# Softmax denominators of the masked layers: two products with ones instead of eight transposes and a reduction

## The chip, the cores and the metric

The kernel runs on one core of a Trainium2 chip. The metric is the time of one launch on the device, in microseconds, as the median of three runs. Beside it stands one profiled execution, from which all rows, waits and timelines below are taken.

The core has a matrix engine (TensorE; PE in the profile, PEld for its weight loads), a vector engine (VectorE, DVE), a scalar engine (ScalarE, ACT), GpSimd (POOL) and a queue engine (SyncE, SP) that issues transfers. SBUF is the on-chip memory of 128 partitions, PSUM the accumulator memory in which TensorE leaves its results.

## The reference

Four cross-attention layers run in a row on 2048 queries of 256 channels, all attending to the same 1601 context rows of 512. Layers 0, 2 and 3 are masked, with 16 heads of 64; layer 1 is grouped, with 16 query heads of 16 on 4 key heads. Each masked layer computes

```python
logits = jnp.einsum('bhqd,bhkd->bhqk', q, k) * scale
logits = logits + col_bias[None, None, :, :]
probs = jax.nn.softmax(logits, axis=-1)
out = jnp.einsum('bhqk,bhkd->bhqd', probs, v)
out = out.transpose(0, 2, 1, 3).reshape(B, HW, HEADS * HEAD_DIM)
out = out @ Wo + bo
out = out + residual
```

`col_bias` lowers a few key columns for the queries that a mask leaves out. The denominator of the softmax is the sum over the 1601 keys of the exponentials, one number for each query and head. All is in 32-bit floats.

## The kernel before, in words

**Tiling.** A unit of a masked layer is two heads and 512 queries (`QB`). Its scores are kept with the keys on the partitions: 13 chunks (`NT`) of up to 128 keys, each chunk a tile of 128 partitions by 2 heads by 512 queries. A masked layer has 8 pairs of heads (a block, with its weights) by 4 groups of queries, so the three masked layers have 96 units. The grouped layer has 4 blocks by 4 groups, and works differently: it makes its scores twice and gets its denominators from a column of ones in the values.

**The steps of a masked unit.** For each chunk, `masked_scores` (L713) makes the scores in a PSUM tile `s`, ScalarE copies it to a tile `p` in SBUF (L725), and VectorE takes the running maximum over the chunks (L730). After the last chunk `maxima` turns the maxima by eight transposes (L773), reduces them on VectorE (L774), and sends them by way of DRAM to all partitions. Five steps later the exponentials begin: VectorE subtracts the maximum (L804), ScalarE takes the exponential (L809), and GpSimd adds the chunk to the tile `sums` (L812, L814), 128 partitions by 2 heads by 512 queries. Two steps behind that, TensorE multiplies with the values into the PSUM tile `po` (L849), the two heads side by side in 64 columns each.

**After the last values** the unit needs its denominators, on all partitions, to divide `oT`, the evicted `po`. `denominators` (L887 to L898) takes a PSUM tile of the scores' pool, transposes `sums` into it in eight pieces, so that queries stand on the partitions and the 128 partial sums along the row, reduces that on VectorE (L891) and takes the reciprocal (L892). Then `on_all_partitions` writes the columns to DRAM (L676) and reads them back as rows broadcast to 64 partitions for each head (L679) into the tile `by`. `divide` multiplies on GpSimd (L912), and `project` multiplies with Wo on TensorE (L920) and adds the result to `xs` on VectorE (L932).

**PSUM.** The pool of the score tiles has two tiles of two banks each while masked layers run. A third tile (`b`) holds the subtracted maxima, one bank is `po`, and one bank (`pm`, here the shared bank) serves all the pieces that make keys, values and queries. Where the grouped layer is being exponentiated, the scores' pool is six single banks instead.

**The order of the work.** The program is written out step by step, two steps (a pair) at a time, and TensorE, ScalarE and VectorE keep the written order; GpSimd and SP are put in order by a scheduler when the program is built. In a pair stand the subtractions, the scores of two chunks, the exponentials, the values of two chunks, and then the pieces of `Pieces`. A piece has a cost and a flag `shared` (it uses the shared bank). Some pieces are due at a fixed number of steps after a unit's last values (`finish`); the others, which make the next block's keys and values, fill pairs:

```python
        def pair(self, steps, pairs):

            cost, taken = self.own(steps)
            many = len(self.fill) + len(self.later) > pairs
            while self.fill and not taken and (many or not cost):
```

A due piece with a cost keeps fillers out of its pair unless many are left; a shared one keeps them out always. The denominators, the division and the projection of a masked unit are due 2, 5 and 10 steps after its last values. SP issues nearly all transfers, in one order: context slices (L262), weights (L440), x (L703), and the two legs of `on_all_partitions` for the denominators and for the maxima.

Of the kernel before, what the change touches and what calls it, by code (L numbers as in the profile page):

```python
# [10 lines left out]
FP = mybir.dt.float32  # L11
# [3 lines left out]
ALU = mybir.AluOpType  # L15
AX = mybir.AxisListType
PSUM = bass.MemoryType.PSUM

P = 128
QB = 512  # L20
# [6 lines left out]
Piece = namedtuple("Piece", "run cost shared", defaults=(True,))  # L27
# [7 lines left out]
def tile_cross_attention_stack(ctx: ExitStack, tc: tile.TileContext, t: dict, out: bass.AP):  # L35
# [31 lines left out]
    nc = tc.nc  # L67
# [6 lines left out]
    NB = S // QB  # L74
    QT = QB // P
# [13 lines left out]
    work = ctx.enter_context(tc.tile_pool(name="work", bufs=2))  # L89
    small = ctx.enter_context(tc.tile_pool(name="small", bufs=2))  # L90
    dram = ctx.enter_context(tc.tile_pool(name="dram", bufs=1, space=bass.MemoryType.DRAM))
    ps_o = ctx.enter_context(tc.tile_pool(name="ps_o", bufs=1, space=PSUM))
    ps_m = ctx.enter_context(tc.tile_pool(name="ps_m", bufs=1, space=PSUM))
    scores_pools = ctx.enter_context(ExitStack())

    ident = const.tile([P, P], FP, name="ident")
    make_identity(nc, ident)
    ones = const.tile([P, P], FP, name="ones")
# [39 lines left out]
    psum = Scores()  # L138
# [351 lines left out]
    class Grouped:  # L490
# [5 lines left out]
        name = "L1_xattn_"  # L496
# [168 lines left out]
    def columns(q):  # L665


        return slice(q, QB, QT)

    def on_all_partitions(cols, to):  # L670


        n = cols.shape[1]
        rows = dram.tile([4, P, QT], FP, name="cols", bufs=4)[:n]
        with nc.allow_non_contiguous_dma(reason="1024 values, four at a time"):
            nc.sync.dma_start(out=rows.rearrange("h p q -> p h q"), in_=cols)  # L676
        for tile_, heads_ in to:
            src = rows[heads_].rearrange("(o h) p q -> o (h p q)", o=1)
            nc.sync.dma_start(out=tile_, in_=src.to_broadcast(tile_.shape))  # L679


    class Unit:
# [191 lines left out]
        def last(self):  # L874
            return self.sub == len(self.layer.SUBS) - 1

        def denominators(self):

            rden = small.tile([P, len(self.pair), QT], FP, name="rden")
            if self.masked:  # L880
                h = 0
                for pt in psum.heads(False)[0]:
                    of = range(h, h + pt.shape[1])
                    pt = pt.rearrange("p h (q k) -> p h q k", k=P)
                    for h in of:
                        for q in range(QT):
                            nc.tensor.transpose(  # L887
                                pt[:, h - of[0], q, :], self.sums[:, h, columns(q)], ident
                            )
                    h += 1  # L890
                    nc.vector.tensor_reduce(rden[:, of[0] : h, :], pt, AX.X, ALU.add)  # L891
                nc.vector.reciprocal(rden, rden)  # L892
            else:
                nc.vector.reciprocal(rden, self.dens)
            self.by = work.tile([P, QB], FP, name="by", bufs=1)
            on_all_partitions(
                rden,
                [(self.by[self.rows(h)], slice(h, h + 1)) for h in range(len(self.pair))],  # L898
            )
# [74 lines left out]
        def finish(self):  # L974

            if self.very_last:
                return [(0, Piece(lambda: self.quarters(of[len(units) - 2]), 2.0))]
            if self.final:

                found = [  # L980
                    (4 if self.b == NB - 2 else 2, Piece(self.denominators, 1.0, False)),
                    (7, Piece(self.divide, 0.0)),
                ]
                if self.b < NB - 2:
                    found.append((10 - 2 * self.b, Piece(self.project_rows, 2.0, False)))
                return found
            if not self.masked:
                return [
                    (1, Piece(self.den_columns, 0.0)), (3, Piece(self.denominators, 0.0)),
                    (6, Piece(self.divide, 0.0)), (8, Piece(self.project, 2.0, False)),  # L990
                ]
            return [
                (2, Piece(self.denominators, 1.0, False)), (5, Piece(self.divide, 0.0)),
                (10, Piece(self.project, 2.0, False)),
            ]


# [4 lines left out]
    for b in range(NB):  # L1002
        nc.scalar.dma_start(
            out=x_rows[b], in_=x[0, ts(b, QB), :].rearrange("(n p) c -> p n c", p=P)
# [10 lines left out]
    of = {}  # L1015
# [343 lines left out]
```

## Time and profile before

| What | us |
|---|---|
| Median of three runs | 4742.91 (4740.15 to 4749.87) |
| Profiled execution, its own time | 4745.24 |
| Span of that execution, first to last instruction | 4743.5 |
| TensorE busy in the span | 4596.3 (97%) |
| VectorE busy | 3744.2 (79%) |
| ScalarE busy | 3226.5 (68%) |
| GpSimd busy | 2977.4 (63%) |

The granted TensorE clock was 0.992 over the span. A row of a group of instructions gives its line, engine and operation, the tiles that it writes and reads (out<-in), its shape and count, then its busy time in us and the mean duration of one in ns, and after the last bar the idle time of that engine just before such instructions with what ended it. In a timeline the columns are start and duration in us, engine, line, operation, tiles, shape and how many of them are merged; brackets give idle time ahead of the row and what ended it. TensorE's ends are modelled and its matmuls overlap, so times on it are best read from start to start.

### The profile page before, as it was taken

How to read it: one execution, taken by the hardware profiler on the slowest of the kernel's cores; microseconds unless marked ns; L12 is line 12 of the kernel's file. 1: busy time of each engine (PE TensorE's matmuls, PEld its weight loads, DVE VectorE, ACT ScalarE, POOL GpSimd, SP SyncE). 2: the span in 40 equal slices, each digit the busy share in tenths (PEclk: the TensorE clock that was granted, in tenths of full speed). 3: DMA queues.
4: the chain of work that ended last, by engine and by line, in shares of the span. 5: the costliest groups of instructions: out<-in, count | busy, mean ns of one | idle time of the engine just before them, and what ended most of it. 6: DMA issues, size and time to landing. Idle time of an engine off the chain costs nothing.

```text
span 4743.5 us, 64047 instructions
## 1 busy us (share of the span) xinstructions
PE 4596.3 (97%) x23943; PEld 1914.1 (40%) x23943; DVE 3744.2 (79%) x3768; ACT 3226.5 (68%) x4013; POOL 2977.4 (63%) x1436
## 2 busy tenths in 40 slices
PE   8999999999989999999999999999999999999998
PEld 5444444444433333343444444344444444444433
DVE  5888888888876666653788888888888888888887
ACT  4777777777635555555677777777777777777776
POOL 3777777778730000000677777777777777777787
PEclk9999999999989999999999999999999999999999
DMA  4322323222201010021232232222232223232211
GB/s 150 85 84 79 88 77 86 81 80 78 74 27 38 20 29 21 20 61 39 79 89 84 78 89 78 84 80 82 76 91 73 86 81 85 75 86 77 84 36 39
DMA packets 349892, 337.63 MB, mean 71 GB/s; under 512 B 116421, under 2 KB 305381, under 8 KB 349580
## 3 DMA queue, kind: packets, MB, share of 16 engines
q1 hardware_dynamic: 346310, 328.14, 24.6%
q8 instruction: 189, 3.10, 0.3%
q0 software_dynamic: 1152, 3.28, 0.2%
q10 hardware_dynamic: 2118, 2.10, 0.1%
q14 instruction: 123, 1.01, 0.1%
HBM read 318.49 MB, written 14.69 MB: 70 GB/s over the span
## 4 chain that ended last, share of the span: by engine, by line
PE 87%; DVE 10%; issue 1%; ACT 1%; POOL 0%; DMA 0%; another core or an unknown queue 0%; ACTq 0%; DVEq 0%; POOLq 0%
PE po L849 28%; PE s L713 20%; PE t L744 9%; PE pm L413 7%; PE pm L459 6%; PE pm L483 4%; PE s L920 4%; DVE rden L891 2%; PE s L887 2%; DVE ntop L774 2%; DVE xs L932 2%; PE s L773 2%; DVE top L730 1%; DVE p L804 1%; PE t L819 1%
## 5 line engine op out<-in xcount | busy, mean ns | idle before, releaser
L814 POOL TENSOR_TENSOR sums<-sums,p 128x1024 f32<-128x1024 f32 x1145 | 2711.0, 2368 | 736.8 <-ACT p L809 566.0
L725 ACT COPY p<-s 128x1024 f32<-128x1024 f32 (+1 forms) x1248 | 1234.2, 1014 | 655.3 <-PE s L713 567.6
L804 DVE TENSOR_TENSOR p<-p,b 128x1024 f32<-128x1024 f32 (+1 forms) x1248 | 1461.2, 1210 | 55.5 <-ACT b L799 54.4
L849 PE MATMUL po<-p,v 128*64 128x512 f32 (+3 forms) x8320 | 1493.5, 522 | 4.9 <-ACT p L809 2.6
L730 DVE TENSOR_TENSOR top<-s,top 128x1024 f32<-128x1024 f32 (+1 forms) x1056 | 1291.4, 1223 | 234.1 <-ACT p L725 171.3
L713 PE MATMUL s<-q,kT 64*128 64x512 f32 (+1 forms) x4992 | 1336.7, 629 | 85.9 <-DVE ntop L774 23.2
L809 ACT ACTIVATE p<-p 128x1024 f32<-128x1024 f32 (+1 forms) x1248 | 1254.7, 1057 | 43.8 <-DVE p L804 42.6
L849 PEld LDWEIGHTS po<-p,v 128*64 128x64 f32 (+3 forms) x8320 | 365.7, 125 | 1115.8 <-issue 889.3
L713 PEld LDWEIGHTS s<-q,kT 64*128 64x128 f32 (+1 forms) x4992 | 388.6, 181 | 722.7 <-issue 215.5
L831 ACT ACTIVATE p<-t 128x512 f32<-128x512 f32 (+1 forms) x760 | 413.8, 594 | 297.6 <-PE t L819 256.5
L757 DVE TENSOR_REDUCE row_top<-t 128x1 f32<-128x512 f32 x700 | 451.2, 686 | 196.8 <-PE t L819 165.2
L912 POOL TENSOR_TENSOR oT<-oT,by 128x512 f32<-128x512 f32 x111 | 141.6, 1276 | 656.4 <-DMA by<-cols 336.1
L819 PE MATMUL t<-q,kT 32*128 32x512 f32 (+1 forms) x1520 | 489.1, 643 | 0.0
L744 PE MATMUL t<-kT,q 32*128 32x512 f32 (+1 forms) x1880 | 481.9, 553 | 0.0
L413 PEld LDWEIGHTS pm<-wv,ct 128*128 128x128 f32 (+1 forms) x2600 | 300.4, 187 | 130.4 <-issue 69.0
L413 PE MATMUL pm<-wv,ct 128*128 128x128 f32 (+2 forms) x2600 | 333.3, 281 | 1.7 <-ACT vs L417 0.7
L459 PE MATMUL pm<-ct,wk 128*128 128x256 f32 (+1 forms) x1344 | 316.7, 379 | 5.4 <-ACT ct L284 4.3
L774 DVE TENSOR_REDUCE ntop<-s 128x8 f32<-128x1024 f32 x96 | 117.6, 1225 | 228.4 <-PE s L773 228.4
L459 PEld LDWEIGHTS pm<-ct,wk 128*128 128x128 f32 x1344 | 232.2, 191 | 161.1 <-issue 99.3
L744 PEld LDWEIGHTS t<-kT,q 32*128 32x128 f32 x1880 | 182.5, 185 | 163.1 <-issue 96.7
L799 ACT COPY b<-spread 128x1024 f32<-128x1024 f32 x96 | 97.5, 1015 | 150.9 <-DVE p L804 150.0
L920 PE MATMUL s<-oT,wo 128*128 128x512 f32 x376 | 187.4, 621 | 2.8 <-DVE row_top L757 1.7
(176 smaller groups left out, 2249.8 us busy)
## 6 DMA issues: line engine op xcount, KB each, us to landing
ct<-ctxT SPq DMA_DIRECT2D x288, 512.0 KB
xT<-xT SPq DMA_DIRECT2D x100, 512.0 KB
spread<-cols SPq DMA_DIRECT2D x96, 512.0 KB
by<-cols SPq DMA_DIRECT2D x190, 128.0 KB
xT<-xs SPq DMA_DIRECT2D x16, 512.0 KB
ct<-ctxT SPq DMA_DIRECT2D x48, 130.0 KB
wk<-in_L_xattn_Wk_dram SPq DMA_DIRECT2D x24, 256.0 KB
wv<-in_L_xattn_Wv_dram SPq DMA_DIRECT2D x24, 256.0 KB
```

The source lines that it names most:

```text
L413: nc.tensor.matmul(pv[:md, d, :f], ct(k)[:, d * P : d * P + md], wv[:, k, :], start=(k == 0), stop=(k == NCT - 1),)
L459: nc.tensor.matmul(pk, u.wk[:, k, :], ct(k), start=(k == 0), stop=(k == NCT - 1))
L713: nc.tensor.matmul(s[:m, h, :], self.u.kT[r, a : a + m], self.q[r, :], start=True, stop=(a != TAIL),)
L725: nc.scalar.copy(p[:m], s[:m])
L730: nc.vector.tensor_tensor(self.top[:m], s[:m], self.top[:m], ALU.max)
L744: nc.tensor.matmul(s[:, at : at + n], self.q[r, ts(q, P)], self.u.kT[r, a : a + n], start=True, stop=True,)
L757: nc.vector.tensor_reduce(self.top[:, of, q, k : k + 1], s, AX.X, ALU.max)
L804: nc.vector.tensor_tensor(self.p[c][:m], self.p[c][:m], self.less[:m], ALU.add)
L809: nc.scalar.activation(p[:m], p[:m], AF.Exp)
L814: nc.gpsimd.tensor_tensor(self.sums[:m], self.sums[:m], p[:m], ALU.add)
L819: nc.tensor.matmul(s[:m], self.u.kT[r, a : a + m], self.q[r, :], start=True, stop=True)
L849: nc.tensor.matmul(to, v, p, start=(c == 0 and not part), stop=(c == NT - 1 and part != 0))
```

## The change

For the masked layers, `denominators` no longer transposes. A new piece `add_up`, due 2 steps after the last values, multiplies `sums` with a matrix of ones, once for each head, into the shared bank: each head's denominators, as a row of 512, stand then on 64 partitions. ScalarE copies the bank to the tile `by`, and two transfers on SP within SBUF put one row of each head onto the 128 partitions, four values on each, in a tile `den`. `denominators`, now due 4 steps after the last values, takes the reciprocal of that and goes on as before by way of DRAM into `by`; the division is due at 6 instead of 5. In the last block the same three are due at 2 or 4 and then 2 and 4 later. `add_up` is marked as shared with cost 1; `denominators` has cost 0 and is marked as shared (without a cost that keeps nothing out). The very last unit has its own path and is not changed. The grouped layer's path runs as before.

```diff
+        def add_up(self):
+            pt = ps_m.tile([P, QB], FP, name="pm")
+            for h in range(2):
+                nc.tensor.matmul(
+                    pt[self.rows(h), :], ones[:, :64], self.sums[:, h, :], start=True, stop=True
+                )
+            self.by = work.tile([P, QB], FP, name="by", bufs=1)
+            nc.scalar.copy(self.by, pt)
+            self.dens = small.tile([P, 2, QT], FP, name="den", bufs=1)
+            with nc.allow_non_contiguous_dma(reason="512 values, four at a time"):
+                for h in range(2):
+                    r = self.rows(h).start
+                    nc.sync.dma_start(
+                        out=self.dens[:, h, :],
+                        in_=self.by[r : r + 1, :].rearrange("o (p q) -> o p q", q=QT),
+                    )
+
         def denominators(self):

             rden = small.tile([P, len(self.pair), QT], FP, name="rden")
-            if self.masked:
-                h = 0
-                for pt in psum.heads(False)[0]:
-                    of = range(h, h + pt.shape[1])
-                    pt = pt.rearrange("p h (q k) -> p h q k", k=P)
-                    for h in of:
-                        for q in range(QT):
-                            nc.tensor.transpose(
-                                pt[:, h - of[0], q, :], self.sums[:, h, columns(q)], ident
-                            )
-                    h += 1
-                    nc.vector.tensor_reduce(rden[:, of[0] : h, :], pt, AX.X, ALU.add)
-                nc.vector.reciprocal(rden, rden)
-            else:
-                nc.vector.reciprocal(rden, self.dens)
-            self.by = work.tile([P, QB], FP, name="by", bufs=1)
+            nc.vector.reciprocal(rden, self.dens)
+            if not self.masked:
+                self.by = work.tile([P, QB], FP, name="by", bufs=1)
             on_all_partitions(
...
+                at = 4 if self.b == NB - 2 else 2
                 found = [
-                    (4 if self.b == NB - 2 else 2, Piece(self.denominators, 1.0, False)),
-                    (7, Piece(self.divide, 0.0)),
+                    (at, Piece(self.add_up, 1.0)), (at + 2, Piece(self.denominators, 0.0)),
+                    (at + 4, Piece(self.divide, 0.0)),
                 ]
...
             return [
-                (2, Piece(self.denominators, 1.0, False)), (5, Piece(self.divide, 0.0)),
-                (10, Piece(self.project, 2.0, False)),
+                (2, Piece(self.add_up, 1.0)), (4, Piece(self.denominators, 0.0)),
+                (6, Piece(self.divide, 0.0)), (10, Piece(self.project, 2.0, False)),
             ]
```

## The prediction, made before the changed kernel had run

> **What bounds the kernel now.** I read the page's shares first, then the groups by shape, then the timeline of one unit. The page's busy row and its chain that ended last:
>
> ```profile
> PE 4596.3 (97%) x23943; PEld 1914.1 (40%) x23943; DVE 3744.2 (79%) x3768; ACT 3226.5 (68%) x4013; POOL 2977.4 (63%) x1436
> ...
> PE 87%; DVE 10%; issue 1%; ACT 1%; POOL 0%; DMA 0%; another core or an unknown queue 0%; ACTq 0%; DVEq 0%; POOLq 0%
> ```
>
> TensorE carries 87% of the chain, VectorE 10%. Shares are averages, so the groups (shapes apart; busy us, mean ns) give the prices:
>
> ```profile
> L849 PE MATMUL po<-p,v 128*64 128x512 f32 x4608 | 1132.5, 608 | 3.9 <-ACT oT L871 2.2 <-ACT p L809 1.6
> ...
> L887 PE MATMUL s<-ident,sums 128*128 128x128 f32 x752 | 115.6, 297 | 3.7 <-DVE top L730 2.2 <-DVE row_top L757 1.4
> ...
> L891 DVE TENSOR_REDUCE rden<-s 128x8 f32<-128x1024 f32 x94 | 115.1, 1225 | 21.2 <-PE s L887 20.9
> ...
> L871 ACT COPY oT<-po 128x512 f32<-128x512 f32 x111 | 64.7, 583 | 4.0 <-PE po L849 4.0
> ```
>
> 752 transposes are 94 units of 8. (Of 96 masked units, the very last has its own path, and one falls in the stretch with single banks.) A product of 64 columns in full precision has two records, so x4 below is two products. The timeline of TensorE around one unit's denominators:
>
> ```profile
> 1033.15 1.99 PE L713 MATMUL s<-q,kT 64*128 64x512 f32 x8
> 1035.07 1.94 PE L849 MATMUL po<-p,v 128*64 128x512 f32 x8
> 1036.94 1.23 PE L887 MATMUL s<-ident,sums 128*128 128x128 f32 x8
> 1038.10 1.13 PE L713 MATMUL s<-q,kT 64*128 64x512 f32 x4
> 1039.49 1.13 PE L713 MATMUL s<-q,kT 64*128 64x512 f32 x4 [0.26 <-DVE rden L891]
> 1040.55 1.94 PE L849 MATMUL po<-p,v 128*64 128x512 f32 x8
> ...
> 1049.32 1.11 PE L773 MATMUL s<-ident,top 128*128 128x128 f32 x8
> ```
>
> TensorE never rests except in that 0.26. The scores of a pair take 1.92 from start to start without denominators (1033.15 to 1035.07), and 3.61 with them (1036.94 to 1040.55): the second scores wait for the score slot that the transposes filled and VectorE must reduce. The block of transposes therefore costs 1.69 us of the bound engine, not its 1.23 of busy time. VectorE in the same stretch:
>
> ```profile
> 1035.43 2.55 DVE L730 TENSOR_TENSOR top<-s,top 128x1024 f32<-128x1024 f32 x2 [0.20 <-ACT p L725]
> 1038.21 1.22 DVE L891 TENSOR_REDUCE rden<-s 128x8 f32<-128x1024 f32 x1 [0.23 <-PE s L887]
> 1039.47 0.20 DVE L892 RECIPROCAL rden<-rden 128x8 f32<-128x8 f32 x1
> ...
> 1046.53 2.54 DVE L730 TENSOR_TENSOR top<-s,top 128x1024 f32<-128x1024 f32 x2
> ```
>
> VectorE ends its maxima at 1049.07, just ahead of the transposes of the maxima (L773) at 1049.32: slack 0.25. That is the place where a late VectorE would stop TensorE.
>
> [...] L849 records last 608 ns each, but eight take 1.87. [...] SP's waits view shows it:
>
> ```profile
> SPq L679 <- DMA cols<-rden: 201.6, 111, 3.2
> ```
>
> A mean wait of 1.8 and at most 3.2, after an issue of 0.37: a small scattered transfer lands some 2.2 us after its issue starts, 3.6 at worst. [...]
>
> **The change part by part.** I set the start of the old transposes at 0.
>
> TensorE: the transposes and their split of the scores go (1.69). In comes a group of two 128x512 products with ones, four records. The very last unit already runs such groups between value products:
>
> ```profile
> 4724.23 1.03 PE L862 MATMUL pm<-p,ones 128*64 128x512 f32 x4
> 4725.09 1.03 PE L849 MATMUL po<-p,v 128*64 128x512 f32 x4
> ```
>
> From start to start 0.86. As half of an x8 value group it is 0.94, by L849's mean 0.98. I take 0.93. The shared bank is free: in this unit's pair of steps there is no other piece, and the previous one was evicted at 1033.6. The sums are ready: the old transposes wait for the same tile at the same place. Gain 1.69 − 0.93 = 0.76 per unit, 94 × 0.76 = 71.4 us.
>
> The new piece is marked as shared, so a filling piece may be displaced. In the two programs as built, TensorE's order differs so in one place only (a values piece after the grouped layer, then two back to back): about 1 us. The alternation of score tiles there shifts too; I count nothing, as the same products run.
>
> ScalarE gains 94 copies of 128x512 at 0.58 (L871) = 55 us. It has 32% free; the copy stands after the pair's exponentials, which end at 1038.22 (+1.28), so it runs to +1.86, and the next scores are not there before +1.9. Hidden; without that cover it would delay one score copy by at most 0.6.
>
> VectorE loses L891 with the gap before it: 1037.98 to 1039.59, 1.61 between the two users, and gets one reciprocal (0.20) a pair later: −1.4 per unit. Not on the bound, worth nothing by itself, but it is the slack that the new wait uses.
>
> SP gains two issues per unit (the grouped layer's same transfer takes a median of 594 ns), at +1.9 and +2.5. SP otherwise stands waiting there (704 us for the reciprocals in all). The second lands at about +4.7 (2.2 after its issue), +6.1 at worst. The reciprocal's place on VectorE is behind the next pair's maxima: 1044.35 − 1.61 − 1036.94 = +5.8. So it normally finds its data. Below: a landing sooner gains nothing.
>
> Behind a late reciprocal stand the subtractions and maxima of the next pair, and then L773. VectorE would end those at 1049.07 − 1.61 + 0.20 = 1047.66; TensorE needs them at 1049.32 − 0.76 = 1048.56. Slack 0.90, so the reciprocal may start until +6.7 at no cost. In alternate units the tail's maximum comes first in its pair (it ends at 1011.80, L773 starts at 1013.93), so there it may start until about +8.6.
>
> Then the issue of the columns (+6.0), landing +8.2, the two broadcast issues (0.55 each, two in 1.11) to +9.3, landing about +11.5. The other loads now put between them on SP (weights, context, x) wait for a piece of TensorE that ends before +6.7. GpSimd's division stands at +10.7 before. In half of the units it now stands one or two additions (2.37 each) later and waits for nothing; in the others it stays, would run at +10.0 and waits 1.5 us. Cover: GpSimd's work in a unit is 13 steps at about 2.37 plus 1.28, some 31.1 of about 38 us, and the projection comes at +23 to +24. Cost nothing; without the cover, at most 1.5 × 47 = 70 us.
>
> The profiled execution took 4745.24 (span 4743.5), 2.3 above the median 4742.91; the sum, −71.4 + 1, is taken off the median: 4742.9 − 70 = 4673 us.
>
> **Rivals.**
> (a) The full gain: 4673; its own range 4655 to 4690 from 0.6 to 0.9 us per unit.
> (b) More: with 1.4 us less on VectorE, other waits shrink too. The waits of the scores for L774 and L932 (23.2 and 20.9 us) are reductions on the same slots and remain, but the last block has no filling pieces, and TensorE waits 0.49 for maxima there. At most some 25 more: 4648.
> (c) The small transfers land 5 us after the second issue (+7.5): TensorE loses 0.8 at L773 in half of the units, and half of the gain: 4673 + 47 × 0.8 = 4711. Against it: the longest wait of the like transfer.
> (d) Slower: the same wait, larger[...]. It decides where the reciprocal starts after +8.2: 47 × (8.2 − 6.7) = 71 us, the gain; that is a landing 5.7 us after the second issue. At 6.5 (+9.0) the price is 47 × 2.3 + 47 × 0.4 = 127: 4800. For it: the grouped layer's use leaves some 10 us before its reciprocal, so no row excludes it. Against it: the 2.2 above.
> (e) TensorE is not the bound between the modelled ends and the freed time turns up as waits: 4743. Against it: the 0.26 shows by name, and groups with no wait join end to start.
>
> **How the numbers follow.** Chances: (a) 0.64, (b) 0.10, (c) 0.13, (d) 0.09, (e) 0.04. Within 0.2% (9.5 us, about what a measurement can tell from no change) is (e). Faster 0.87, same 0.04, slower 0.09. The range 4645 to 4714 holds (a), (b) and most of (c).
>
> **What would show it.** L887 and L891 gone for the masked layers; scores x8 in about 1.92 after a ones group of about 0.93 with no wait; the 22.9 us of L713 on rden gone; VectorE's reciprocal with little or no idle time on the transfer; division on GpSimd waiting 1 to 2 us in half of the units; the unit 0.76 shorter. Wrong if the reciprocal shows a wait over 1 us on the transfer and L773 waits for top L730 behind it, or if SP's broadcast issues slip beyond +12 and the projection waits for the division.

## The result, and the profile after

| What | Predicted | Measured |
|---|---|---|
| Median, us | 4673 (4645 to 4714) | 4677.95 (4672.7 to 4681.14, four runs) |
| Kernel before beside it, us | | 4746.39 (4740.15 to 4751.68, four runs) |
| Ratio to before | | 0.9855, 95% interval 0.9838 to 0.9872 |
| Span of the profiled execution, us | | 4671.0 (before 4743.5) |

The kernel is 68 us faster by the medians, 72.5 by the two spans; the profiled execution of the changed kernel is the fastest of its four runs. The page's busy row and its chain after the change:

```profile
PE 4549.1 (97%) x23563; PEld 1854.4 (40%) x23563; DVE 3617.7 (77%) x3672; ACT 3263.2 (70%) x4108; POOL 2983.8 (64%) x1436
...
PE 90%; DVE 7%; issue 1%; ACT 1%; POOL 0%; DMA 0%; another core or an unknown queue 0%; ACTq 0%; SPq 0%; DVEq 0%; POOLq 0%
```

TensorE's share of the chain rises from 87% to 90% and VectorE's falls from 10% to 7%: L891, which had 2% of it, is gone. TensorE's timeline around the same unit's denominators:

```profile
1011.86 1.99 PE L713 MATMUL s<-q,kT 64*128 64x512 f32 x8
1013.78 1.94 PE L849 MATMUL po<-p,v 128*64 128x512 f32 x8
1015.55 1.03 PE L882 MATMUL pm<-sums,ones 128*64 128x512 f32 x4
1016.50 1.99 PE L713 MATMUL s<-q,kT 64*128 64x512 f32 x8
1018.42 1.94 PE L849 MATMUL po<-p,v 128*64 128x512 f32 x8
...
1027.15 1.12 PE L773 MATMUL s<-ident,top 128*128 128x128 f32 x8
```

The scores now run as one x8 group, without the 0.26 wait. From one value group's start to the next it is 4.64 us (1013.78 to 1018.42), where in the kernel before it was 5.48 (1035.07 to 1040.55): 0.84 less. For the whole trace I take as the length of a unit the time from its denominators on TensorE (the transposes, now the products) to those of the next unit. Regular units have a short and a long length in turn. The medians are now 35.52 and 40.73 us; in the kernel before they were 36.35 and 41.60. That is 0.83 and 0.87 less. VectorE in the same stretch:

```profile
1018.87 2.55 DVE L730 TENSOR_TENSOR top<-s,top 128x1024 f32<-128x1024 f32 x2
1021.33 0.19 DVE L899 RECIPROCAL rden<-den 128x8 f32<-128x8 f32 x1
1021.44 2.30 DVE L804 TENSOR_TENSOR p<-p,b 128x1024 f32<-128x1024 f32 x2
1023.66 2.54 DVE L730 TENSOR_TENSOR top<-s,top 128x1024 f32<-128x1024 f32 x2
```

The reciprocal starts 5.8 us behind the products (1021.33 − 1015.55) with no wait, and the maxima end at 1026.20 (1023.66 + 2.54), 0.95 us ahead of L773. The groups by shape show the wait for the transfer over the whole program, and the waits view shows GpSimd's for the broadcast:

```profile
L899 DVE RECIPROCAL rden<-den 128x8 f32<-128x8 f32 x95 | 18.4, 193 | 3.0 <-DMA den<-by 3.0
```

```profile
POOL oT L918 <- DMA by<-cols: 549.8, 65, 62.0
```

One reciprocal of 95 waited, for 3.0 us. GpSimd now waits 65 times for the broadcast; in the kernel before it waited 11 times (336.1 us). Most of either total lies in the grouped layer, where single waits reach 60 us. Between 130 and 1100 us, in the first masked layer, 25 divisions run, and the profile names 12 waits of 30.8 us in all. Ahead of 7 more divisions GpSimd stands idle for 19.1 us, which the profile puts down to ScalarE or TensorE. In the kernel before no division of that stretch had idle time ahead of it.

### The profile page after: what moved, and what is told of

The parts are those of the page before. It is cut to its first block, busy times and chain, and to the rows that moved or that the text cites. A ratio compares the mean times of both kernels' runs of the same rounds, so it can differ in the third digit from the quotient of the medians.

```text
span 4671.0 us, 63856 instructions
## 1 busy us (share of the span) xinstructions
PE 4549.1 (97%) x23563; PEld 1854.4 (40%) x23563; DVE 3617.7 (77%) x3672; ACT 3263.2 (70%) x4108; POOL 2983.8 (64%) x1436
## 4 chain that ended last, share of the span: by engine, by line
PE 90%; DVE 7%; issue 1%; ACT 1%; POOL 0%; DMA 0%; another core or an unknown queue 0%; ACTq 0%; SPq 0%; DVEq 0%; POOLq 0%
PE po L849 29%; PE s L713 22%; PE t L744 9%; PE pm L413 7%; PE pm L459 6%; PE s L926 4%; PE pm L483 4%; DVE ntop L774 2%; DVE xs L938 2%; PE s L773 2%; PE pm L882 2%; PE t L819 1%; DVE top L730 1%; DVE p L804 1%; PE pm L595 1%
## 5 line engine op out<-in xcount | busy, mean ns | idle before, releaser
L804 DVE TENSOR_TENSOR p<-p,b 128x1024 f32<-128x1024 f32 (+1 forms) x1248 | 1460.8, 1209 | 55.2 <-ACT b L799 52.9
L713 PE MATMUL s<-q,kT 64*128 64x512 f32 (+1 forms) x4992 | 1312.3, 626 | 63.5 <-DVE ntop L774 23.2
L713 PEld LDWEIGHTS s<-q,kT 64*128 64x128 f32 (+1 forms) x4992 | 400.6, 182 | 727.6 <-issue 312.3
L774 DVE TENSOR_REDUCE ntop<-s 128x8 f32<-128x1024 f32 x96 | 117.6, 1225 | 254.9 <-PE s L773 250.7
```

What stands on the lines that cost most here:

```text
L713: nc.tensor.matmul(s[:m, h, :], self.u.kT[r, a : a + m], self.q[r, :], start=True, stop=(a != TAIL),)
L804: nc.vector.tensor_tensor(self.p[c][:m], self.p[c][:m], self.less[:m], ALU.add)
```

## The experiments

Every ratio is to the kernel before, run in the same job on the same chip. The changed kernel's own ratio was 0.9855, and in three more jobs 0.9847, 0.9849 and 0.9835. Unit lengths are medians of the regular units, as above.

### VectorE's reduction put back alone

```diff
+            idle = small.tile([P, 2, QT], FP, name="idle", bufs=1)
+            nc.vector.tensor_reduce(
+                idle, self.sums.rearrange("p h (q k) -> p h q k", k=P), AX.X, ALU.add
+            )
             self.by = work.tile([P, QB], FP, name="by", bufs=1)
             nc.scalar.copy(self.by, pt)
```

> The changed kernel with VectorE's reduction of 128x1024 put back, as an extra instruction that reads the sums in SBUF and whose result nobody uses; no score tile and no TensorE work go with it. Theory (the gain is TensorE's own time and the score tile that VectorE held): VectorE comes 1.2 us later to the next pair; the slack ahead of the transposes of the maxima is about 0.95 us in half of the units of the changed kernel, so at most 0.3 x 47 = 14 us are lost: 4678 to 4695 us. Rival (the gain came from the 1.4 us per unit that VectorE was relieved of): most of the 68 us are lost, 4735 us or more.

Measured: 4695.79 us, ratio 0.9868 (0.9851 to 0.9885). The extra instruction takes 1209 ns, 95 times. Unit lengths are 35.52 and 41.02 us: nothing in one half of the units, 0.29 in the other. VectorE's relief of 1.4 us per unit is thus not what the gain of the regular units is made of; the rival falls. The loss has the size that was expected from the slack of 0.95 us ahead of L773, but it does not arise at L773. In a unit of the longer kind, with its products at 1019.39, TensorE's timeline is:

```profile
1025.17 2.35 PE L713 MATMUL s<-q,kT 64*128 64x512 f32 x8
1027.35 0.38 PE L720 MATMUL s<-bias_rows,tail_keys 64*65 64x512 bf16 x2
```

These scores, of the pair of steps that holds the short last chunk, take 2.18 us from start to start, where in the changed kernel they took 1.82 (1021.33 to 1023.15). Behind them L773 starts at 1031.35, and the maxima have ended 0.19 us earlier. The row of the last chunk's shape names what TensorE waits for; its idle time was 0.4 us in the changed kernel:

```profile
L713 PE MATMUL s<-q,kT 64*65 64x512 f32 x384 | 103.1, 614 | 7.1 <-DVE top L730 4.5
```

A late VectorE thus stops TensorE first at the score tiles, which come free late, and only then at L773.

### The products twice

```diff
-            for h in range(2):
+            for h in (0, 1, 0, 1):
                 nc.tensor.matmul(
                     pt[self.rows(h), :], ones[:, :64], self.sums[:, h, :], start=True, stop=True
                 )
```

> The changed kernel with each of the two products with ones made twice into the same place. Theory (TensorE sets the pace, so its time counts in full): a group of two products costs 0.86 to 0.97 us, times 94 units: 81 to 91 us more, 4759 to 4769 us, which is above the kernel before. Rival (TensorE has room and VectorE sets the pace): less than 20 us more.

Measured: 4758.37 us, ratio 1.0006 (0.9997 to 1.0014), where the changed kernel has 0.9855: some 72 us more by the ratios. The span is 4751.9, 80.9 us above the changed kernel's. (The kernel before was some 9 us slower in this job than in the first, so the medians of the two jobs are not compared, and the spans only roughly.) Unit lengths are 36.38 and 41.59 us: 0.86 more in each kind, which is 81 us for 94 units and the low end of the theory; the ratios give somewhat less. The timeline of TensorE in that kernel:

```profile
998.38 1.89 PE L882 MATMUL pm<-sums,ones 128*64 128x512 f32 x8
1000.20 1.99 PE L713 MATMUL s<-q,kT 64*128 64x512 f32 x8
```

In the regular units TensorE's time counts in full, and a group of two products costs 0.86, not 0.93. With one such group more the whole gain is gone: the kernel before and this one have the same unit lengths within 0.03.

### The products in a score tile

```diff
-            pt = ps_m.tile([P, QB], FP, name="pm")
+            pt = psum.heads(False)[0][0][:, 0, :]
```

> The changed kernel with the products written into a tile of the scores' pool, as the transposes were, and evicted from there by the same copy on ScalarE. Theory (what cost time was VectorE holding the tile until 2.5 us after the start of the transposes): ScalarE empties it at about +1.9, when the second scores are due at +2.0, so little is lost, 0 to 0.2 us per unit: 4678 to 4697 us. Rival (any use of a score tile costs the whole wait and split of about 0.5 us per unit): about 4725 us.

Measured: 4700.61 us, ratio 0.9881 (0.9865 to 0.9898). Unit lengths are 35.77 and 40.98 us, 0.25 more than the changed kernel, so just above the range of the theory and far from the rival. TensorE's timeline:

```profile
1021.33 1.04 PE L882 MATMUL s<-sums,ones 128*64 128x512 f32 x4
1022.53 1.99 PE L713 MATMUL s<-q,kT 64*128 64x512 f32 x8 [0.16 <-DVE top L730]
```

The scores no longer split, and what they wait for is not the copy that empties the products' tile. With one more tile in the turn, the next scores meet the tile of the scores just before, which VectorE's maximum still reads. So of the 0.86 us, 0.25 belongs to taking a turn of the score tiles, even where ScalarE empties the tile soon. The other 0.61 belongs to the transposes' longer work and to the reduction that held their tile; this run does not separate these two.

### The reciprocal at once

```diff
-                (2, Piece(self.add_up, 1.0)), (4, Piece(self.denominators, 0.0)),
+                (2, Piece(self.add_up, 1.0)), (2, Piece(self.denominators, 0.0)),
```

(The same with `at` in the last block.)

> The changed kernel with the reciprocal (and the two legs after it) due in the same pair of steps as the products, so that VectorE waits for the transfers within SBUF in plain view. Theory: the second transfer lands 2.2 us after its issue starts, some 4.7 us after the products start, and VectorE, free at about +1.0, waits some 3.5 us per unit; TensorE then loses about 2.9 us in one half of the units and 1.8 in the other, since the next scores need the score tiles: about 220 us more, 4900 us (4820 to 4960). Rival (the transfer lands within about 1 us, or VectorE has more room than I think): under 4720 us.

Measured: 4963.91 us, ratio 1.0437 (1.0419 to 1.0454), span 4966.5. The waits view of this kernel, and VectorE's and TensorE's timelines in one unit (products at 999.62):

```profile
DVE rden L899 <- DMA den<-by: 332.2, 95, 5.4
```

```profile
1004.89 0.20 DVE L899 RECIPROCAL rden<-den 128x8 f32<-128x8 f32 x1 [4.12 <-DMA den<-by]
```

```profile
1004.36 1.09 PE L413 MATMUL pm<-wv,ct 128*65 128x128 f32 x8
1008.50 3.79 PE L713 MATMUL s<-q,kT 64*128 64x512 f32 x8 [3.04 <-DVE top L730]
1012.07 0.64 PE L720 MATMUL s<-bias_rows,tail_keys 64*65 64x512 bf16 x2
1012.64 2.71 PE L849 MATMUL po<-p,v 128*64 128x512 f32 x8
```

The mean wait is 332.2/95 = 3.5 us, as the theory had it. In this unit the two issues of the transfers run from 1001.50 to 1002.64, so the second starts near 1002.07 and the reciprocal starts on its data at 1004.89: 2.8 us. Rival (d) of the prediction is thus a real mechanism: with no cover, the wait reaches TensorE by way of the score tiles. The loss is larger than expected (span 295 us above the changed kernel's, against about 220), and differently spread: 1.91 and 4.11 us per unit, where 1.8 and 2.9 were expected. The unit shown is of the second kind and one of the longest (46.50 us; the median is 44.84). TensorE stands for 3.04 us in it and then runs slowly: eight scores take 3.57 us (1008.50 to 1012.07) instead of 1.92. The windows view of TensorE, whose last columns are granted clock, DMA share and GB/s, shows the slower clock:

```profile
1004.00:1008.00 4.00, 1.45 (x11) 0.93 0.04 1
1008.00:1012.00 4.00, 3.50 (x8) 0.50 0.69 178
1012.00:1016.00 4.00, 4.00 (x14) 0.72 0.26 87
1016.00:1020.00 4.00, 3.74 (x17) 1.00 0.39 131
```

After the stop the clock is 0.50 for 4 us and 0.72 for the next 4. In that time these scores take 1.65 us more and the values behind them 0.77 (2.64 from start to start in place of 1.87).

Most units of the second kind stand for about 2.3 us. In 4 of the 37 regular ones the clock stays full behind that stop (1.00), as here, by the timeline and the windows view:

```profile
2608.76 1.13 PE L713 MATMUL s<-q,kT 64*128 64x512 f32 x4 [2.36 <-DVE top L730]
```

```profile
2608.00:2612.00 4.00, 3.04 (x14) 1.00 0.57 139
```

These four take 43.45 to 43.64 us, 2.7 to 2.9 above the changed kernel's 40.73: the loss that was expected. The median of this kind, 44.84, is 4.11 above. So what the expectation lacked is the fall of the clock, to 0.50 in the unit shown first. Over the whole span the mean granted clock was 0.973, and 0.991 in the changed kernel. As an estimate from these, 0.027 × 4966.5 − 0.009 × 4671.0 = 92 us of the 295 go to the clock, which leaves about 203 for the waits.

### The division later

```diff
-                (6, Piece(self.divide, 0.0)), (10, Piece(self.project, 2.0, False)),
+                (8, Piece(self.divide, 0.0)), (10, Piece(self.project, 2.0, False)),
```

> The changed kernel with the division due 8 steps after the last values instead of 6 (not in the last block), so that GpSimd no longer waits for the broadcast, some 3 us in half of the units. Theory (GpSimd makes that up before anybody needs it): the same time within 8 us, and GpSimd's waits for the broadcast in the masked layers nearly gone. Rival (GpSimd's wait holds back score copies on ScalarE, whose tiles it frees): 10 to 50 us faster.

Measured: 4680.31 us, ratio 0.9848 (0.9831 to 0.9864), unit lengths 35.52 and 40.73 us as without the edit. But the edit did not do what it was for: GpSimd's order is made by the scheduler, the division kept its place 12 to 15 us behind the products, and in the stretch from 130 to 1100 us it still waits 12 times, 25.8 us in place of 30.8. So this says nothing on what GpSimd's wait is worth. That it costs TensorE nothing in a regular unit rests on TensorE's timeline of the changed kernel alone, where the two waits of 0.26 left in a unit (for L774 and for L938) name VectorE.

### Where 8 us went: the stretch after the grouped layer

About 94 units at 0.86 give 81 us, and the spans differ by 72.5. Most of what is missing lies where the last units of the grouped layer run between the scores of the next masked layer. From the last queries made while the grouped layer still runs, the first unit length (here from one unit's queries to the next unit's) was 63.8 us in the kernel before and is 70.6 in the changed one. TensorE's windows over that length, of the kernel before and of the changed one:

```profile
2158.36:2222.18 63.82, 59.01 (x405) 1.00 0.09 29
```

```profile
2133.34:2203.91 70.57, 63.90 (x406) 0.93 0.08 25
```

The clock was full in the first and 0.93 in the second. The score tiles come in another order there: the turns are counted, some work takes the tile `b` at every third turn, and the old denominators counted one turn for each unit. I took the order for the cause, and ran the changed kernel again with two tries at restoring it.

> The changed kernel as it is, beside the two others of this call, to see what of its trace repeats. In the first trace the regular units gave 0.86 us each and some 8 us were lost around the grouped layer, 6.75 of them in the 70.6 us between the last query projections of that stretch, where the granted clock fell to 0.93 for the whole stretch. Theory (the loss comes from the order of the score tiles, which is part of the program): the same stretch takes 69 to 72 us again. Rival (the fall of the clock there is chance): it takes 64 to 66 us in this trace. Time 0.9855 of the kernel before, within 0.2%.

Measured: 4678.89 us, ratio 0.9847 (0.983 to 0.9863); first length 72.2, the one behind it (second length) 64.1 (first trace 70.6 and 60.0); all regular units as before to 0.01 us.

```diff
         def add_up(self):
+            psum.turn += 1
             pt = ps_m.tile([P, QB], FP, name="pm")
```

> The changed kernel with one line more, which counts a turn of the score tiles for each products piece, as the old denominators did; TensorE's order in the mixed stretch after the grouped layer is then that of the kernel before. Theory (the lost 6.75 us come from the shifted tiles: two more waits of 1.5 and 0.3 us, and a clock that falls behind them): that stretch takes 64 to 65 us as before, and the time falls by 4 to 7 us against the changed kernel. Rival (chance, or the copy on ScalarE and the new transfers): no difference within 3 us.

Measured: 4685.13 us, ratio 0.9853 (0.9831 to 0.9875); lengths 76.3 and 70.4. The try was a miss: it counts a turn also for the one unit that runs with single banks, and so makes a third order. With that mended:

```diff
         def add_up(self):
+            if not psum.banks:
+                psum.turn += 1
             pt = ps_m.tile([P, QB], FP, name="pm")
```

> The changed kernel with a turn of the score tiles counted for each products piece, but only while score tiles go in pairs, as the old denominators counted it. (The earlier try counted one turn too many, so that its order in the mixed stretch was a third one, neither that of the kernel before nor that of the changed one.) TensorE's order after the grouped layer is now that of the kernel before. Theory (the order of the tiles there makes TensorE wait and the granted clock fall): the first of the two unit lengths after the grouped layer takes 64 us, as in the two kernels so far with this order (63.8 and 63.9), not 70 to 80 as in the five traces without it; the whole is 5 to 10 us faster than the changed kernel beside it. Rival (chance): a length of 70 us or more, and no difference above 4 us.

> The changed kernel as it is, on the same chip as the run before it, for comparison: the first unit length after the grouped layer 70 us or more (by theory), regular units 35.52 and 40.73 us again.

Measured: 4666.44 us (0.9828, 0.9815 to 0.9842) with the turn, 4674.7 (0.9849, 0.9835 to 0.9863) without; first lengths 63.8 and 70.6, as the theory had it, but second lengths 65.7 and 60.0. So I repeated both.

> The kernel with the turn counted as before, once more beside the changed kernel, because the first comparison was 8.3 us in time, while the two traces differed by 6.7 us in the first unit length after the grouped layer, by 5.8 us the other way in the second, and for the rest at the start and the end of the program. Theory (the order of the tiles is worth time): again 5 us or more faster than the changed kernel beside it, first length 64 us. Rival (the clock's falls are chance and the earlier difference was the draw of one job): within 4 us of it.

> The changed kernel as it is, beside the run before it. Theory: first unit length after the grouped layer 70 us or more again. Rival: about 64 us.

Measured: 4675.63 us (0.9843, 0.9825 to 0.9861) with the turn, 4663.78 (0.9835, 0.9816 to 0.9855) without; first lengths 77.3 and 77.0. The theory falls: the same order has given 63.8 and 77.3, and the changed kernel alone ranges from 4662 to 4685 us over its runs.

The waits show how little the order itself costs. Over the first and second lengths together, TensorE's waits in the timeline sum to 11.45 us in the kernel before, and to 11.88 in each of the four traces of the changed kernel: the other order moves 1.9 us of waiting into the first length and 1.4 out of the second. Yet in these four traces the two lengths together take 130.6, 136.3, 130.6 and 142.6 us (124.3 in the kernel before), and the clock over the first length is 0.93, 0.91, 0.93 and 0.84. What differs from trace to trace is where the clock falls. In the changed kernel's first trace it is behind a wait of 1.51 for a maximum at 2164.15; the kernel before has a wait of 1.51 in that length too (before 2197.13), and its clock stays full, as the windows of the two show, changed kernel first:

```profile
2162.00:2166.00 4.00, 2.49 (x18) 1.00 0.00 0
2166.00:2170.00 4.00, 4.00 (x16) 0.53 0.00 0
2170.00:2174.00 4.00, 4.00 (x22) 0.50 0.00 0
```

```profile
2195.00:2199.00 4.00, 2.49 (x18) 1.00 0.00 0
2199.00:2203.00 4.00, 4.00 (x28) 1.00 0.01 0
```

The stop (1.51 us) and TensorE's busy time in its window (2.49 of 4 us) are equal in the two, the clock behind them is 0.53 in one and 1.00 in the other. With the reciprocal at once it was 0.50 behind the stop of 3.04 us shown above and 1.00 behind that of 2.36. So the length of a stop alone does not tell a fall, and what sets one off is not shown. It stays open, too, whether the new kernel loses some us in this stretch on average, since of the kernel before there is one trace. For the whole program the runs hint at it. In the three later jobs in which both kernels ran, the mean granted clock was 0.9885, 0.9894 and 0.9900 in the changed kernel and 0.9901, 0.9910 and 0.9904 in the kernel before. In the last of these jobs the runs at a clock of 0.992 took 4739.06 us in the kernel before and 4662.23 and 4663.78 in the changed one, 75 to 77 us apart.

## Why the prediction was right

**The total.** 4673 was predicted and 4677.95 measured, 70 us of gain against 68. That is closer than its two terms, whose errors cancel: the regular units gave 81 us where 71 were counted, and the mixed stretch took more back than the 1 us counted. So the mechanism was right, and the last 2 us of agreement are luck. The ratios of the other three jobs, 0.9835 to 0.9849, stand for 72 to 78 us.

**TensorE's price per unit.** Predicted 1.69 − 0.93 = 0.76, measured 0.83 and 0.87. The mis-sized term is the products: 0.86 by the experiment that doubled them. That is the price between the value groups of the very last unit, one of the three shown (0.86, 0.94 and 0.98); averaging it with the two that come from half of a value group was the error. 94 × 0.86 = 81 us.

**The wait for VectorE's reduction** (the 0.26 and the split) is gone, and reading 1.69 us as more than the 1.23 of busy time was right. Of the 0.86 gained, 0.61 is had even with the products in a score tile; the other 0.25 comes from taking no turn of those tiles.

**The new wait.** Predicted: the reciprocal's place at +5.8, the data at +4.7, no wait. The place was +5.8, the transfer took 2.8 instead of 2.2 us in the one unit that shows it (with the reciprocal at once), and one reciprocal waited. Slack ahead of L773: predicted 0.90, measured 0.95. But L773 is not the first place where a late VectorE stops TensorE: with the reduction put back it was the scores one pair of steps earlier. Rivals (c) and (d) stayed out for the reason given, and the run without the cover shows that their mechanism was the right one to fear. The price expected for that run (220 us against 295) left out the slower clock behind a stop (0.50 in the unit shown), as the prices of (c) and (d) do.

**GpSimd's wait for the broadcast** was predicted as 1.5 us in half of the units. In the first masked layer it is 30.8/12 = 2.6 us in about half of them, with idle time of another name in 7 more. The broadcasts' landing was mis-sized: in the unit with products at 980.20, the two issues start at 989.52 (+9.3 instead of +8.2), and the division starts at 993.67, +13.5 instead of +11.5. The wait is hidden, as far as TensorE's timeline shows. The sum of GpSimd's work in a unit was written down wrongly: 13 × 2.37 + 1.28 is 32.1, not 31.1. As the first of the 13 steps is a copy of 1.04 us, it is 12 × 2.37 + 1.04 + 1.28 = 30.8, so the cover was there.

**The rest.** Rival (b), more than the units' own gain where VectorE sets the pace, showed in the last block: four units gained 1.28 to 1.49 us each in place of 0.86, some 2 us more in all, too few to matter. With the reduction put back alone, the same four lose 0.32 to 1.08 us again, so there VectorE's relief does count. The moved values piece cost 1.3 us where 1 was counted. For the shifted score tiles I counted nothing. The trace lost about 6 us in the two lengths there (130.6 against 124.3); the order of the tiles accounts for 0.4 us of waiting, and by the repeats it is not shown to be the cause of the rest.

## What to carry to other kernels

On the engine that sets the pace, price an operation from start to start of its neighbours, not by its busy time: the transposes were busy 1.23 us and cost 1.69, because they took a turn in a pool of two tiles that the next work needed, and VectorE held their tile. A new wait on a transfer cost nothing here, where what waits was placed one pair of steps later, behind the landing; the same wait one pair earlier cost four times the gain (295 us of span against 72.5). Before a difference of 0.2% is put down to a change of order, run the unchanged program as often as the changed one.

## What the runs showed of the hardware that was not expected

A stop of TensorE can cost more than its length: after 3.04 us of waiting, the granted clock was 0.50 for the next 4 us and 0.72 for the 4 after, and the work behind it took 2.4 us longer. Of the 37 regular units of that kind, which mostly stood for about 2.3 us, 4 kept the full clock and took 43.45 to 43.64 us, where the median was 44.84. Behind a stop of 1.51 us the clock was 0.53 in one trace and 1.00 in another. And regular work repeats to 0.01 us from trace to trace (median unit lengths of 35.52 and 40.73 in all four traces of the changed kernel, taken in different jobs), while the whole scatters by some 20 us (4662 to 4685) with the mean granted clock: 0.992 in the fastest of these runs, 0.987 in the slowest.
